# A selective scan fed from GpSimd: one product per unit over both of its pairs, stores of y two units later, one tile of sums for the whole program

## The chip, the cores and the metric

The program runs on one core of one Trainium2 chip. The metric is the device time of one execution in microseconds. The kernel before takes 13546.32 us (median of 3 runs, 13542.6 to 13555.92). A profiled execution of the same kernel took 13547.65 us, of which 13545.9 us lie between its first and its last instruction (the span).

A core has five instruction streams that run side by side and meet only at semaphores: PE (TensorE, matrix products), DVE (VectorE), ACT (ScalarE), POOL (GpSimd) and SP (SyncE, which here issues every DMA). Each stream works in order: an instruction that waits holds up all that stand behind it on its engine.

## The reference: what is computed

The input x is 16 images of 256 channels by 32 x 32 places. Layer 0 adds a transformer block (group norm, layer norms, attention of 4 heads, a GELU layer). Layer 1 adds a Mamba block with a gate. What this change touches is the scan in layer 1:

```python
def step(h, inp):
    d_t, B_t, C_t, u_t = inp
    dA = jnp.exp(d_t[..., None] * A)
    h = dA * h + (d_t * u_t)[..., None] * B_t[:, None, :]
    y = jnp.einsum('bdn,bn->bd', h, C_t)
    return (h, y)
```

It runs over 1024 places for 512 inner channels with 64 states each, for every image: `h` has 512 x 64 values, and at each place it is multiplied by a decay, gets the product (d_t u_t) B_t added, and is summed against C_t over the 64 states to give y.

## The kernel before, in words

**Units.** The scan of one image is cut into 256 units (line 38): two blocks of 512 places (t), four blocks of 128 channels (k), four groups in each (q), eight units in a group (i). A unit has two pairs, e = 0 and 1; the 128 partitions of a pair hold 64 states of 2 channels, and its 512 columns are the places. There are 16 x 256 = 4096 units. I call the group of eight units (b, t, k, q) a group.

For a unit n five things happen:

- `load(n)` (line 838, the DMA at line 859): SP issues one DMA of 512 KB that brings d_t u_t of the unit's channels from DRAM to the tile `dub`, 128 x 2 x 512, each row spread over 64 partitions. `dub` has 7 buffers (`dutp`).
- `inputs(n)` (line 865): GpSimd multiplies each half `dub[:, e, :]` by `bt` (B of the block t, 128 x 512) in place, in two instructions of 128 x 512 (line 869).
- `decay(n)` (line 871): PE forms the exponents in PSUM (line 878), ACT takes the exponential (line 881) into the tiles `a`, of which there are four, that is two units' worth.
- `scan(n, e)` (line 883): VectorE runs the recurrence as one `tensor_tensor_scan` per pair (line 891), from `a` in PSUM and the half of `dub`, into `h`.
- `outputs` (line 915), once per group: PE multiplies `h` by C (`cd`) into the left half of the PSUM tile `yb` (line 928), ACT copies it to `y2` (936), PE turns it into the right half of `yb` (940), ACT copies that to `yo` (948), SP stores it to DRAM in four DMAs of 16 KB (954). It is a generator: it is advanced by one `yield` per unit, so that its parts are spread over the units of the next group. The first part runs at the unit with i = 0, the stores at that with i = 6.

**The loop** over units (from line 974) writes the instructions of one unit after the other: `load(n + 6)`, `inputs(n + 4)`, the two scans of n, `decay(n + 2)`, a share of the side work, then one step of `outputs`. Each compute engine is held to this order (the loop at line 1059 ties every instruction to the one before it on its engine); SP's order follows it closely.

**Side work.** While image b is scanned, the next image is prepared a step at a time: `first_norm`, `attention_layer` and `scan_inputs` of b + 1, and `gate_and_store` of b - 1. The steps are spread evenly over the 256 units. Some of their VectorE instructions read two operands from SBUF: lines 330 (add the position), 515 and 539 (attention), 584, 642 and 682 (the convolution and its gate), 787 and 791 (the gate on y). Others have one operand in PSUM.

**The turn from one image to the next.** At the unit with (k, q, i) = (0, 0, 6) `spread_c` lays out C: GpSimd clears the tile `cd` (128 x 4096, line 903, at t = 0 only), and ACT then writes 8 strided pieces into it (line 907). In GpSimd's order the clearing stands behind the products up to unit 10 of the new image. In ACT's order the exponential for the first group norm of the following image (line 261) stands behind the pieces of `cd`, and VectorE's line 264 needs that exponential.

**Sums.** `yb` (128 x 512 in PSUM, one buffer) is allocated anew for each (b, t), 32 times, and its right half is cleared by VectorE each time (line 918), since PE writes only 16 of every 32 rows of it.

The last image has no following image to prepare: beside its scan only `gate_and_store` of image 14 runs.

Of the kernel before, what the change touches and what calls it, by code (L numbers as in the profile page):

```python
# [11 lines left out]
F32 = mybir.dt.float32  # L12
BF16 = mybir.dt.bfloat16
AF = mybir.ActivationFunctionType
ALU = mybir.AluOpType
# [4 lines left out]
P = 128  # L20
# [3 lines left out]
HL = 512  # L24
# [9 lines left out]
TB = 512  # L34
# [18 lines left out]
def attention_then_scan_kernel(  # L53
# [18 lines left out]
    nc = tc.nc  # L72
    B = x.shape[0]

    def pool(name, bufs, **kw):
        return ctx.enter_context(tc.tile_pool(name=name, bufs=bufs, **kw))
# [13 lines left out]
    yps = pool("yps", 1, space=PSUM)  # L90
# [11 lines left out]
    def work(name, n=L):  # L102
        return wide.tile([P, L + 2 + CONV], F32, name=name, tag="wide")[:, :n]
# [12 lines left out]
    def col(name, i=0, n=1):  # L116
        o, w = _COLS[name]
        assert i + n <= w
        return vec[:, o + i : o + i + n]
# [59 lines left out]
    t = work("ones_s")[:1]  # L179
# [3 lines left out]
    for k in range(KC):  # L183
        t = work("rel_s").rearrange("p (i j) -> p i j", j=32)
        rh = col("rel_h", 32 * k, 32).unsqueeze(1).to_broadcast([P, 32, 32])
        rw = col("rel_w", 32 * k, 32).unsqueeze(2).to_broadcast([P, 32, 32])
        nc.vector.tensor_copy(t, rh)
        nc.vector.tensor_tensor(t, t, rw, ALU.add)
        nc.sync.dma_start(rel[ts(k, P), :], t)


    def weights(*specs):
# [643 lines left out]
    blocks, loaded, decays = {}, {}, {}  # L836
    now = {}
# [26 lines left out]

    def inputs(n):
        b, t = units[n][:2]
        for e in range(2):
            v = loaded[n][:, e, :]
            nc.gpsimd.tensor_tensor(v, v, blocks[b, t]["bt"], ALU.mult)  # L869

    def decay(n):
        b, t, k, q, i = units[n]
# [40 lines left out]


    def outputs(b, t, k, q):
        if (k, q) == (0, 0):
            now["yb"] = yps.tile([P, HL], F32, name="yb", tag="yb")
            nc.vector.memset(now["yb"][:, 256:], 0.0)  # L918
        cd, yb, hbuf = now["cd"], now["yb"], now["h", q % 2]
        out4 = yb[:, 256:].rearrange("p (j a m e) -> p a e j m", a=2, j=2, e=4)  # L920
        if t == 0:
            nc.scalar.copy(now["last"][:, ds(64 * k + 16 * q, 16)], hbuf[:, :, TB - 1])
        for half in range(2):
            for s in range(4):
                for c in range(4):
                    for g in range(4):
                        at = 128 * s + 64 * half + 16 * g + 4 * c
                        nc.tensor.matmul(  # L928
                            yb[ts(g, 32), ts(s, 64)],
                            cd[:, at // 16, ts(c, 32)], hbuf[:, :, at : at + 4],  # L930
                            start=(c == 0), stop=(c == 3),
                        )
                if s == 1:
                    yield
            y2 = blk.tile([P, 256], F32, name="y2", tag="y2")
            nc.scalar.copy(y2, yb[:, :256])  # L936
            yield
            for e in range(4):
                for s in range(4):
                    nc.tensor.matmul(  # L940
                        out4[32 * s : 32 * s + 16, half, e],
                        y2[:, 64 * s + e : 64 * s + 64 : 4], turn[:, e],
                        start=True, stop=True,
                    )
            if half == 0:
                yield
        yo = blk.tile([P, 256], F32, name="yo", tag="yo")
        nc.scalar.copy(yo, yb[:, 256:])
        yield
        to = state[b]["ys"][ds(k * P + 32 * q, 32), ts(t, TB)].rearrange(  # L950
            "(j i) (s c) -> s i j c", j=2, s=4
        )
        for s in range(4):
            nc.sync.dma_start(  # L954
                to[s], yo[32 * s : 32 * s + 16].rearrange("p (j c) -> p j c", j=2)
            )
# [10 lines left out]
    for n in range(LEAD):  # L967
        inputs(n)
# [4 lines left out]
    for n, (b, t, k, q, i) in enumerate(units):  # L973
# [19 lines left out]
        if n + LEAD < len(units):  # L993
            inputs(n + LEAD)
# [11 lines left out]
        if i == 0 and n > 0:  # L1006
            g = outputs(*units[n - 1][:4])
            next(g)
            running.append(g)
# [5 lines left out]
    for _ in outputs(*units[-1][:4]):  # L1015
        pass
# [71 lines left out]
```

## Time and profile before

| | |
|---|---|
| median of 3 runs | 13546.32 us |
| profiled execution | 13547.65 us |
| its span | 13545.9 us |
| VectorE busy | 12092.7 us, 89% |
| PE busy | 10672.8 us, 79% |
| GpSimd busy | 10483.0 us, 77% |
| ScalarE busy | 7925.4 us, 59% |
| mean granted TensorE clock | 0.766 |
| GpSimd products, line 869 | 8192 of 1.307 us |
| scans, line 891 | 8192 of 1.202 or 1.261 us |

How to read it. The first scan starts 388 us into the span: before that the first image is prepared with nothing beside it. From there 15 images take 801 to 836 us each, 3.2 us a unit, and the last image 676 us; 46 us follow the last scan. The busy share of an engine counts instructions from start to end; instructions that follow each other directly on VectorE and GpSimd overlap in the record, so that two scans, of 1.2 us each, are written down as 2.3 to 2.46 us for both. A product that waits for its port is written down as a longer product.

### The profile page before, as it was taken

What the parts mean: (1) busy time and instruction counts of PE and PEld (TensorE: products, weight loads), DVE (VectorE), ACT (ScalarE), POOL (GpSimd) and SP (SyncE); (2) the same over time, 40 slices, a digit from 0 to 9 for tenths busy, and PEclk for the clock granted to TensorE, in tenths of its full rate; (3) what the DMA queues carried; (4) which work ended last, traced back from release to release, by engine and by line L of the source; (5) the groups of instructions that cost most, each with busy time, mean ns of one, the idle gap of its engine ahead of it and who ended that gap; (6) DMA issues with size and microseconds to landing.
All of it is one profiled execution on the core that took longest, in us unless ns stands there. A gap on an engine that the chain in (4) does not pass through costs nothing. (4 is left out here: it accounts for less than half of the span.)

```text
span 13545.9 us, 437083 instructions
## 1 busy us (share of the span) xinstructions
PE 10672.8 (79%) x186800; PEld 5381.9 (40%) x186800; DVE 12092.7 (89%) x11683; ACT 7925.4 (59%) x13941; POOL 10483.0 (77%) x8214
## 2 busy tenths in 40 slices
PE   7787878878787787877878778787887878878757
PEld 3344344433444334443344434434343343433434
DVE  3899999899998989989898998999988999899898
ACT  3666665656656566655656646566565665656644
POOL 0687878878787787877878778787887877878788
PEclk8786877868688686876868778687786877868767
DMA  1566566665666656656666666656666566665666
GB/s 60 198 208 235 196 215 217 205 229 200 208 217 202 228 200 219 210 202 222 207 230 197 204 219 210 232 195 207 220 204 229 197 215 214 201 231 202 203 218 225
DMA packets 1001958, 2821.36 MB, mean 208 GB/s; under 512 B 175810, under 2 KB 319427, under 8 KB 1000004
## 3 DMA queue, kind: packets, MB, share of 16 engines
q1 hardware_dynamic: 1000004, 2793.39, 61.1%
q8 instruction: 1460, 23.92, 0.7%
q14 instruction: 494, 4.05, 0.1%
HBM read 2514.18 MB, written 261.62 MB: 205 GB/s over the span
## 5 line engine op out<-in xcount | busy, mean ns | idle before, releaser
L869 POOL TENSOR_TENSOR dub<-dub,bt 128x512 f32<-128x512 f32 x8192 | 10428.0, 1307 | 3013.2 <-DMA dub<-dus 2609.3
L881 ACT ACTIVATE a<-a,acol 128x512 f32<-128x512 f32 x8192 | 5070.3, 660 | 3815.8 <-PE a L878 3783.7
L891 DVE TENSOR_TENSOR_SCAN h<-a,last,dub 128x512 f32<-128x512 f32 x4096 | 4928.7, 1261 | 136.2 <-POOL dub L869 76.9
L891 DVE TENSOR_TENSOR_SCAN h<-a,dub 128x512 f32<-128x512 f32 x4096 | 4695.9, 1202 | 287.8 <-POOL dub L869 209.5
L878 PE MATMUL a<-pieces,pick 48*128 48x512 bf16 x8192 | 2967.8, 466 | 2345.9 <-DVE h L891 2265.8
L928 PEld LDWEIGHTS yb<-h,cd 128*32 128x32 f32 x131072 | 2563.5, 135 | 2036.9 <-issue 1671.6
L928 PE MATMUL yb<-h,cd 128*32 128x64 f32 x131072 | 2963.2, 258 | 148.9 <-DVE yb L918 108.3
L878 PEld LDWEIGHTS <-pick 48*128 48x128 bf16 x8192 | 520.9, 96 | 2514.6 <-issue 2312.0
L403 PE MATMUL s_ps<-k,q 32*64 32x512 f32 x4096 | 889.3, 717 | 59.1 <-DVE mx L384 57.9
L940 PEld LDWEIGHTS yb<-turn,y 128*16 128x16 f32 x32768 | 408.8, 119 | 1010.9 <-ACT y L936 473.1
L936 ACT COPY y<-yb 128x256 f32<-128x256 f32 x1024 | 383.7, 375 | 728.9 <-PE yb L928 722.9
L384 DVE TENSOR_REDUCE mx<-s_ps 128x1 f32<-128x512 f32 x1024 | 646.1, 675 | 23.6 <-PE s_ps L403 21.5
L940 PE MATMUL yb<-turn,y 128*16 128x32 f32 x32768 | 538.9, 212 | 107.0 <-ACT y L936 97.2
L471 PE MATMUL st_ps<-sp 33*128 33x512 f32 x2048 | 601.1, 632 | 16.7 <-ACT pt L479 15.0
L459 PE MATMUL av<-pt,vv 128*64 128x512 f32 x2048 | 582.7, 648 | 5.6 <-ACT sums L448 3.3
L479 ACT ACTIVATE pt<-st_ps 128x512 f32<-128x512 f32 x1024 | 557.4, 605 | 48.7 <-PE st_ps L471 47.1
L657 PE MATMUL g_ps<-w,xp 128*128 128x256 f32 x1536 | 447.4, 446 | 0.0
L403 PEld LDWEIGHTS s_ps<-k,q 32*64 32x64 f32 x4096 | 207.0, 148 | 580.3 <-DVE mx L384 541.5
L657 PEld LDWEIGHTS g_ps<-w,xp 128*128 128x128 f32 x1536 | 388.9, 328 | 98.6 <-issue 75.0
L816 PE MATMUL m_ps<-w,xs 128*128 128x256 f32 x1024 | 310.5, 452 | 12.0 <-DVE xs L791 12.0
L642 DVE SCALAR_TENSOR_TENSOR u<-up,cwh,u 128x1024 f32<-128x1024 f32 x192 | 285.0, 1485 | 31.8 <-ACT u L634 31.5
L816 PEld LDWEIGHTS m_ps<-w,xs 128*128 128x128 f32 x1024 | 258.8, 328 | 89.8 <-issue 61.4
(135 smaller groups left out, 7122.9 us busy)
## 6 DMA issues: line engine op xcount, KB each, us to landing
dub<-dus SPq DMA_DIRECT2D x4096, 512.0 KB
dps<-pc SPq DMA_DIRECT2D x384, 128.0 KB
pieces<-dps SPq DMA_DIRECT2D x1024, 48.0 KB
xs<-in_x_dram SPq DMA_DIRECT2D x64, 512.0 KB
xs<-kept SPq DMA_DIRECT2D x64, 512.0 KB
zs<-z SPq DMA_DIRECT2D x64, 512.0 KB
ud<-u SPq DMA_DIRECT2D x64, 512.0 KB
dus<-du SPq DMA_DIRECT2D x64, 512.0 KB
```

The costliest lines, as they stand in the source:

```text
L384: nc.vector.tensor_reduce(mx[:, g, c, hf : hf + 1], s, AX.X, ALU.max)
L403: nc.tensor.matmul(waiting[g][0][ts(e, 64)], q4[r, ts(c, 64)], k4[r, hs(hf)], start=True, stop=True,)
L459: nc.tensor.matmul(av[ts(e, 2 * DH)], vv[j // (NJ // 2)][:, j % (NJ // 2), 2 * pair + e, :], pts[e], start=(j == 0), stop=(j == NJ - 1),)
L471: nc.tensor.matmul(s, ka[r, ts(j, P)], qa[r, hs(hf)], start=True, stop=True)
L657: nc.tensor.matmul(ps[:, ts(q, C)], xp[k][:, ds(first + t, P, 4)], wg_s[:, k, t, :], start=(i == 0), stop=False,)
L816: nc.tensor.matmul(ps[:, ts(q, C)], us[d][:, ds(first, P, 4)], wo_s[:, d, :], start=(d == 0), stop=(d == ND - 1),)
L869: nc.gpsimd.tensor_tensor(v, v, blocks[b, t]["bt"], ALU.mult)
L878: nc.tensor.matmul(a, w, pieces[r], start=True, stop=True)
L881: nc.scalar.activation(a, a, AF.Exp, scale=acol[:, at : at + 1])
L891: nc.vector.tensor_tensor_scan(now["h", q % 2][:, 2 * i + e, :], decays[n][e], loaded[n][:, e, :], first, ALU.mult, ALU.add,)
L928: nc.tensor.matmul(yb[ts(g, 32), ts(s, 64)], cd[:, at // 16, ts(c, 32)], hbuf[:, :, at : at + 4], start=(c == 0), stop=(c == 3),)
L940: nc.tensor.matmul(out4[32 * s : 32 * s + 16, half, e], y2[:, 64 * s + e : 64 * s + 64 : 4], turn[:, e], start=True, stop=True,)
```

## The change

Three edits. `inputs` issues one product of 128 x 1024 for the unit, with `bt` read twice through a broadcast, where it issued two of 128 x 512. The stores of y come two units later (with i = 0 of the group after, ahead of the next `outputs`). `yb` is allocated and cleared once, ahead of everything, in place of 32 times.

```diff
+    yb = yps.tile([P, HL], F32, name="yb", tag="yb")
+    nc.vector.memset(yb, 0.0)
...
     def inputs(n):
         b, t = units[n][:2]
-        for e in range(2):
-            v = loaded[n][:, e, :]
-            nc.gpsimd.tensor_tensor(v, v, blocks[b, t]["bt"], ALU.mult)
+        v, bt = loaded[n], blocks[b, t]["bt"]
+        nc.gpsimd.tensor_tensor(v, v, bt.unsqueeze(1).to_broadcast([P, 2, TB]), ALU.mult)
...
     def outputs(b, t, k, q):
-        if (k, q) == (0, 0):
-            now["yb"] = yps.tile([P, HL], F32, name="yb", tag="yb")
-            nc.vector.memset(now["yb"][:, 256:], 0.0)
-        cd, yb, hbuf = now["cd"], now["yb"], now["h", q % 2]
+        cd, hbuf = now["cd"], now["h", q % 2]
...
         yo = blk.tile([P, 256], F32, name="yo", tag="yo")
         nc.scalar.copy(yo, yb[:, 256:])
-        yield
+        for _ in range(3):
+            yield
         to = state[b]["ys"][ds(k * P + 32 * q, 32), ts(t, TB)].rearrange(
```

## The prediction

> **What bounds the kernel now.** I read the busy times first, then the costliest groups of VectorE and GpSimd, and then, since shares are averages, the order of time at places where one of them idles.
>
> ```profile
> PE 10672.8 (79%) x186800; PEld 5381.9 (40%) x186800; DVE 12092.7 (89%) x11683; ACT 7925.4 (59%) x13941; POOL 10483.0 (77%) x8214
> ...
> L869 POOL TENSOR_TENSOR dub<-dub,bt 128x512 f32<-128x512 f32 x8192 | 10428.0, 1307 | 3013.2 <-DMA dub<-dus 2609.3
> L891 DVE TENSOR_TENSOR_SCAN h<-a,last,dub 128x512 f32<-128x512 f32 x4096 | 4928.7, 1261 | 136.2 <-POOL dub L869 76.9
> L642 DVE SCALAR_TENSOR_TENSOR u<-up,cwh,u 128x1024 f32<-128x1024 f32 x192 | 285.0, 1485 | 31.8 <-ACT u L634 31.5
> ```
>
> VectorE is the bound: of 3.2 us a unit the two scans take 2.3 to 2.46, side work most of the rest. GpSimd has idle time and spends it waiting for loads. By the starts and ends in the trace the product of a unit is complete 12.5 us (median, first 15 images) before its scan starts. So the waits that the list puts down to GpSimd (286.3 us, VectorE's line 891 on line 869) mostly belong to others, and a faster product is worth nothing in the middle of an image. Two places are different.
>
> The first is the turn between images, here to image 5, from the order of time on GpSimd, ACT and VectorE:
>
> ```profile
> 4490.32 44.23 POOL L869 TENSOR_TENSOR dub<-dub,bt 128x512 f32<-128x512 f32 x36 [5.85 <-DMA dub<-dus]
> 4534.47 3.53 POOL L903 MEMSET cd<- 128x4096 f32 x1
> ...
> 4538.03 2.45 ACT L907 ACTIVATE cd<-ct,par 128x128 f32<-128x128 f32 x8 [3.08 <-POOL cd L903]
> ...
> 4544.65 1.22 DVE L264 TENSOR_TENSOR gn<-gn,gn_v_ps 128x1024 f32<-128x1024 f32 x1 [6.03 <-ACT gn_v_ps L261]
> ```
>
> Columns are start, length, instruction, and in brackets the idle time before. GpSimd runs 36 products (18 units) without a pause, clears `cd`, ACT stood 3.08 us for that, and VectorE 6.03 us for ACT. Here GpSimd's pace ends last.
>
> The second is VectorE's instructions with two SBUF operands:
>
> ```profile
> L642 DVE SCALAR_TENSOR_TENSOR u<-up,cwh,u x192: 1250/1274/2374, 282.5 to 12642.2; 128x1024 f32<-128x1024 f32 x192
> ...
> L787 DVE SCALAR_TENSOR_TENSOR xs<-xs,vec x64: 1253/1588/16045, 1245.4 to 13522.4; 128x1024 f32<-128x1024 f32 x64
> ```
>
> ```profile
> 5967.20 1.26 POOL L869 TENSOR_TENSOR dub<-dub,bt 128x512 f32<-128x512 f32 x1
> 5967.49 2.06 DVE L642 SCALAR_TENSOR_TENSOR u<-up,cwh,u 128x1024 f32<-128x1024 f32 x1
> 5968.43 2.26 POOL L869 TENSOR_TENSOR dub<-dub,bt 128x512 f32<-128x512 f32 x1
> ```
>
> The same instruction takes 1.25 us alone (minimum) and up to 2.37 (maximum). In the example it starts 0.97 us before the first product of a unit ends, and ends 1.09 us after that; the second product, begun 0.03 us before the first ends, stretches to 2.26 us. The two engines exclude each other, one instruction at a time, and VectorE gets in **between the two products of a unit**. Line 787's 16 us are another case: four times in the last image it stood behind 12 products in a row, with GpSimd never idle.
>
> ```profile
> 12911.84 15.74 DVE L787 SCALAR_TENSOR_TENSOR xs<-xs,vec 128x1024 f32<-128x1024 f32 x1
> ...
> 12908.12 18.38 POOL L869 TENSOR_TENSOR dub<-dub,bt 128x512 f32<-128x512 f32 x15
> ```
>
> What this exclusion costs now: counts times (mean less minimum) over lines 642, 682, 787, 791, 584, 330, 539 and 515 come to 200 us. Of that four waits of line 787 are 58, and 142 us are ordinary, over 508 instructions, 0.28 us each.
>
> **The change part by part.** The sum is made against the profiled execution, 13547.65 us, 1.3 above the median.
>
> *Length of the merged product.* No row shows 128 x 1024 on GpSimd. Products in a row start 1.226 us apart (44.23 us for 36). Merging saves the fixed part of one instruction. Its shortest instruction, a clearing of one column, takes 0.099 us; its 128-column select takes 0.295, which also holds work on columns. So a merged product takes 2.35 us against 2.45, with ends of 2.16 and 2.45 (nothing saved). I take 2.35: the one-column row is nearest to a pure fixed part. The Trainium skill (GPSIMD Engine Reference, Elementwise) gives 4497 ns for a two-input add of 2048 columns; with the row's 1.27 us for 512 columns an estimate from that page is 2.30 us apart, and the next term would be -41 in place of -27.
>
> *Turns between images.* 18 units times 0.099 us is 1.8 us off the run of products, the clearing comes earlier by that, and with it ACT and VectorE's line 264, or in the last image the scan of its unit 9. ACT waited 62.5 us for the clearing in 15 turns, 4.2 on average, so 1.8 fits in. 15 x 1.8 = **-27 us**; ends 0 and -62. The first scan of a unit now waits for both halves; at the turns the second half ends at worst 0.6 us after the scan's start, and by then the run is 0.7 us ahead, so this costs nothing (at most 15 x 0.6 = 9).
>
> *Exclusion.* An instruction of VectorE that arrives in the first product of a unit gets in after it today; merged, it waits for what was the second as well. By starts and ends in the trace, images 0 to 14 have 472 such instructions: 63 arrive with no product running, 252 in the second product of a unit, 157 in the first. Only the 157 change. All of them with 1.12 us more (the second product less the fixed part) would be 176 us. But 79 of them arrive in the last 0.2 us of the first product: there a run of two products began when the previous such instruction let go, and two scans (2.46) took about as long as the run (2.45). After the merge such a run is one whole product, 2.35 us, and ends before the scans do, so these arrive free. The other 78 pay 1.1 us: **+85 us**, all on the path, as VectorE is the bound. Ends 0 (arrivals all fall in step with the products' ends) and +176. I take the middle value, since it is counted from this trace. The Trainium skill (SBUF, "two separate sides") says the same and speaks against the change: the port pair is an exclusive lock for the whole instruction, the loser fully blocks. By that rule alone, with arrivals at random, the mean wait would go with the product's length, 0.28 to 0.52 us, or +122 us.
>
> *The four long waits.* Between them VectorE's unit takes 2.23 us and GpSimd's 2.45, so GpSimd falls behind and has six units of landed loads to run through. Falling behind by 0.12 instead of 0.22 us a unit, over the some 22 units before each, leaves it one unit less to run, about 2.4 us, and 0.1 for each of the others: 4 x 3 = **-12 us**; ends 0 and -54.
>
> *The tile of sums.* 32 clearings of 0.272 us go, one of 128 x 512 comes (0.485, the row of line 429), in VectorE's order: **-8 us**; ends 0 and -9. PE's 108.3 us of waiting for it (14 times) goes too, but no scan waits for PE there.
>
> *The stores of y.* SP waits 557.6 us for line 948 at the stores; two units later that wait is gone, and loads behind it are issued up to 3 us sooner. The product's lead of 12.5 us hides that today: 0. At the turn the four stores (1.7 us of SP) now stand ahead of the load that starts the run of 36, but SP idles there from 2803.5 to 2807.2 us in the turn to image 3, waiting for line 748. If that cover were gone: 15 x 1.7 = +26. `yo` has two buffers, so its next copy waits for nothing new.
>
> The sum is -27 + 85 - 12 - 8 + 0 = +38 us: 13547.65 + 38, about **13585 us**, 0.29% over the median.
>
> **The rivals.**
> 1. *Exclusion costs nothing more* (faster). VectorE's arrivals settle just after the products' ends, as the medians close to the minimum (1274 against 1250 for line 642) suggest. Against it: means of 1485 and 1497 show that a quarter to a half of them don't. Then -47: 13501 us, and down to 13423 with the other terms at their ends. It decides when the added wait is under about 20 us.
> 2. *VectorE loses the port for a further product.* An arrival within the last 0.1 us of a product already loses to the next one today (the maxima of 2.37 us); a loss would then cost 2.35 us. If half of some 170 arrivals near an end lose, 85 x 2.35 = 200 in place of 85: about 13700 us. Against it: GpSimd mostly has no next load landed (1593 waits for loads).
> 3. *Nothing measurable*: the terms cancel, the exclusion costing 20 to 70 us: 13520 to 13573.
> 4. *The product gets no shorter, or longer*: the -27 and -12 go, 13625 us; at 3.2 us a product or more GpSimd would bound everything.
>
> **How the numbers follow.** A measurement of this kernel can tell about 0.2% (27 us) from no change. I give the forecast with its neighbours above 13573 a chance of 0.40, rival 1 0.27, rival 2 0.12, rival 3 0.18, rival 4 0.03. So faster 0.27, same 0.18, slower 0.55. The range reaches from below rival 1 (its likely part, 13480) to rival 2 (13700); below it and above it I leave about 0.1 each. The forecast's own range, with the exclusion between 60 and 120 us, is 13560 to 13620.
>
> **What would show each step.** In the profile after: 4096 products of about 2.4 us (their mean, with waits, near 2.5); the idle time before line 264 on ACT down from 96.2 us by some 25; the minima of lines 642, 682, 787, 791 unchanged, their means up by 0.15 to 0.3 us and line 642's maximum near 3.5; line 787's longest near 13 us; line 918 once; SP's wait on line 948 near zero. I am wrong if those means don't rise, if the merged product is under 2.23 us (then GpSimd keeps pace in the last image and the four long waits go), or if VectorE's idle time before scans grows.

## The result, and the profile after

The changed kernel takes 13529.56 us (median of 12 runs, 13499.69 to 13552.05) beside 13544.95 for the kernel before in the same session: ratio 0.9988, 95% interval 0.998 to 0.9997. It is about 15 us faster, where 39 us slower was forecast; the range held it, the likeliest case did not. Its profiled execution took 13520.45 us (span 13518.5), 27.2 less than that of before.

In the changed file the quoted side lines stand three lower (642 is 645, 787 is 790, 264 is 267, 515 is 518); the product is line 871, the scan 893, the load 862.

From the page of the kernel after, the busy times and three of the costliest groups:

```profile
PE 10686.8 (79%) x186800; PEld 5389.6 (40%) x186800; DVE 12165.9 (90%) x11652; ACT 7916.0 (59%) x13941; POOL 9761.5 (72%) x4118
...
L871 POOL TENSOR_TENSOR dub<-dub,bt 128x1024 f32<-128x1024 f32 x4096 | 9706.4, 2386 | 3702.5 <-DMA dub<-dus 3218.5
...
L645 DVE SCALAR_TENSOR_TENSOR u<-up,cwh,u 128x1024 f32<-128x1024 f32 x192 | 341.0, 1776 | 32.8 <-ACT u L637 32.5
```

GpSimd does the same work in 722 us less. VectorE is busier, 12165.9 against 12092.7 us: line 645 alone has 56 us more (341.0 against 285.0).

Two-operand lines of VectorE, shortest, median and longest in ns:

```profile
L645 DVE SCALAR_TENSOR_TENSOR u<-up,cwh,u x192: 1250/1522/3484, 271.7 to 12644.1; 128x1024 f32<-128x1024 f32 x192
```

```profile
L790 DVE SCALAR_TENSOR_TENSOR xs<-xs,vec x64: 1250/1768/11680, 1233.4 to 13495.4; 128x1024 f32<-128x1024 f32 x64
```

The minima stand, the medians and the maximum of line 645 rose (1274 to 1522, 2374 to 3484): a merged product is waited for whole. Line 790's longest fell from 16.0 to 11.7 us.

The turn to image 5, from the order of time on GpSimd:

```profile
4488.78 41.62 POOL L871 TENSOR_TENSOR dub<-dub,bt 128x1024 f32<-128x1024 f32 x18 [6.51 <-DMA dub<-dus]
```

18 units take 41.62 us, 2.312 each, where they took 44.23.

VectorE's list of waits (us in total, times, longest), first of the kernel before, then of the kernel after:

```profile
DVE gn L264 <- ACT gn_v_ps L261: 96.2, 16, 7.9
...
DVE ao L515 <- DMA sums<-den: 56.4, 15, 5.5
```

```profile
DVE gn L267 <- ACT gn_v_ps L264: 61.8, 16, 5.3
...
DVE ao L518 <- DMA sums<-den: 11.2, 10, 5.6
```

The first pair is the turn between images, 34 us less. The second pair is in none of the prediction's steps: `ao`, the attention's output divided by its softmax sums, waits 45 us less for these sums to arrive. That is more than the whole difference between the two kernels.

By stages (times between the first scans of the images): before the first scan -10.8 us, images 0 to 14 +11.9, the last image -29.0, after it +0.6. The start-up of the kernels below, in which next to nothing of it is changed, stands -2 to +16 us to that of before from trace to trace; what the -10.8 comes from no run here shows.

What happened around `ao` is read from SP's queue in image 5, where the sums of the softmax are put through DRAM: `den` is written, `few` read, inverted by VectorE, `den` written again, and read into `sums`. First before, then after (start, length, DMAs that SP issues):

```profile
5763.28 0.55 SPq L496 DMA_DIRECT2D few<-den  x1
5764.68 1.71 SPq L954 DMA_DIRECT2D ys<-yo  x4
5766.43 0.52 SPq L859 DMA_DIRECT2D dub<-dus  x1
5768.19 0.34 SPq L505 DMA_DIRECT2D den<-few  x1
5770.47 2.87 SPq L859 DMA_DIRECT2D dub<-dus  x2
5773.43 1.93 SPq L508 DMA_DIRECT2D sums<-den  x4
```

```profile
5759.35 0.55 SPq L499 DMA_DIRECT2D few<-den  x1
5761.10 0.52 SPq L862 DMA_DIRECT2D dub<-dus  x1
5761.71 0.55 SPq L954 DMA_DIRECT2D ys<-yo  x1
5764.35 0.34 SPq L508 DMA_DIRECT2D den<-few  x1
5764.74 0.89 SPq L954 DMA_DIRECT2D ys<-yo  x2
5766.66 0.52 SPq L862 DMA_DIRECT2D dub<-dus  x1
5767.27 1.93 SPq L511 DMA_DIRECT2D sums<-den  x4
```

Before, two loads of `dub` stand between `den` and `sums`; after, one load and two stores. A load waits for a scan to free its buffer, so each costs SP about a unit: `sums` is issued 5.24 us after `den` before (5768.19 to 5773.43), 2.92 us after. VectorE meanwhile, of before:

```profile
5767.81 0.35 DVE L503 RECIPROCAL few<-few 128x32 f32<-128x32 f32 x1 [2.81 <-DMA few<-den]
...
5780.72 0.75 DVE L515 TENSOR_TENSOR ao<-ao,sums 128x512 f32<-128x512 f32 x1 [3.00 <-DMA sums<-den]
```

and of after:

```profile
5763.97 0.35 DVE L506 RECIPROCAL few<-few 128x32 f32<-128x32 f32 x1 [2.93 <-DMA few<-den]
...
5774.48 0.75 DVE L518 TENSOR_TENSOR ao<-ao,sums 128x512 f32<-128x512 f32 x1 [0.84 <-DMA sums<-den]
```

Eight scans lie between the two instructions in both kernels. Before, they do not cover the way of the sums (3.00 us idle); after, they nearly do (0.84). Of the other 14 such places, 13 have the same two orders of SP.

### The profile page after: what moved, and what is told of

The parts are those of the page before. It is cut to its first block, busy times and chain, and to the rows that moved or that the text cites. A ratio compares the mean times of both kernels' runs of the same rounds, so it can differ in the third digit from the quotient of the medians.

```text
span 13518.5 us, 429250 instructions
## 1 busy us (share of the span) xinstructions
PE 10686.8 (79%) x186800; PEld 5389.6 (40%) x186800; DVE 12165.9 (90%) x11652; ACT 7916.0 (59%) x13941; POOL 9761.5 (72%) x4118
## 5 line engine op out<-in xcount | busy, mean ns | idle before, releaser
L871 POOL TENSOR_TENSOR dub<-dub,bt 128x1024 f32<-128x1024 f32 x4096 | 9706.4, 2386 | 3702.5 <-DMA dub<-dus 3218.5
L939 PE MATMUL yb<-turn,y 128*16 128x32 f32 x32768 | 538.2, 212 | 103.2 <-ACT y L935 99.4
L645 DVE SCALAR_TENSOR_TENSOR u<-up,cwh,u 128x1024 f32<-128x1024 f32 x192 | 341.0, 1776 | 32.8 <-ACT u L637 32.5
```

The source lines that it names most:

```text
L871: nc.gpsimd.tensor_tensor(v, v, bt.unsqueeze(1).to_broadcast([P, 2, TB]), ALU.mult)
L939: nc.tensor.matmul(out4[32 * s : 32 * s + 16, half, e], y2[:, 64 * s + e : 64 * s + 64 : 4], turn[:, e], start=True, stop=True,)
```

## The experiments

"Ordinary exclusion" below is, as in the prediction, the duration over the minimum, summed over the eight two-operand lines, without waits over 2.5 us ("long waits"), which are counted apart. Before: 142.5 us ordinary, 57.8 in 4 long waits. After: 257.9 and 27.3 in 3.

**One edit alone, and the three with one undone.** e1: only the stores late.

```diff
         nc.scalar.copy(yo, yb[:, 256:])
-        yield
+        for _ in range(3):
+            yield
```

> The kernel before with the stores of y two units later and nothing else. Theory A: this edit moves SP's order in the attention's softmax sums, so that one load fewer stands between the store of the reciprocals and the four loads of the sums; VectorE's wait at line 515 falls from 56.4 us to about 12, and the time by 38 to 45 us, to some 13505 (ratio 0.997). Theory B, that of the prediction: SP's time is hidden, and the time stays (ratio 1.000).

Measured: ratio 0.9973 (0.9963 to 0.9983). VectorE's wait for the sums, in place of the 56.4 us of before:

```profile
DVE ao L515 <- DMA sums<-den: 10.2, 9, 5.5
```

By its trace `ao`'s idle time in images 0 to 14 went from 50.8 to 4.7 us, and these images together are 41.4 us shorter than before (the last image is 20.6 longer, on which more at e4). The stores alone give the gain, and more than the whole change.

e2: only the product merged.

```diff
-        for e in range(2):
-            v = loaded[n][:, e, :]
-            nc.gpsimd.tensor_tensor(v, v, blocks[b, t]["bt"], ALU.mult)
+        v, bt = loaded[n], blocks[b, t]["bt"]
+        nc.gpsimd.tensor_tensor(v, v, bt.unsqueeze(1).to_broadcast([P, 2, TB]), ALU.mult)
```

> The kernel before with the merged product and nothing else. Theory A: +97 us of exclusion in images 0 to 14, -34 us at the turns, -29 us in the last image: +34 us, 13579 (ratio 1.0025), and the wait at line 515 stays at 56 us. Theory B: the longer VectorE instructions cost nothing, because what follows them would have waited anyway, and the freed GpSimd gives the whole gain: -15 to -60 us (ratio 0.996 to 0.999), with line 515's wait down to 11 us as in the changed kernel.

Measured: 1.0047 (1.0032 to 1.0061). Its profiled execution is the slowest of its six, 26 us over their median; in it images 0 to 14 are 103.2 us longer than before, the last image 29.3 shorter. Three lines of its trace, the line of the convolution and two waits:

```profile
L642 DVE SCALAR_TENSOR_TENSOR u<-up,cwh,u x192: 1249/1554/3386, 298.3 to 12761.8; 128x1024 f32<-128x1024 f32 x192
```

```profile
DVE gn L264 <- ACT gn_v_ps L261: 57.9, 16, 5.3
...
DVE ao L515 <- DMA sums<-den: 55.4, 15, 5.6
```

Both halves of the reasoning on the product are in it: line 642 longer (+63 us with its idle time), the turn shorter (96.2 to 57.9), and `ao` as it was. The merged product by itself makes the kernel slower, as forecast.

e3: only one tile of sums (the first and third hunk of the change).

> The kernel before with one tile of sums for the whole program and nothing else. Both theories: -8 to -10 us (ratio 0.9993), no VectorE wait changed. If it is more, PE's 108 us of waiting for the clearing were on the path.

Measured: 1.0003 (0.9991 to 1.0014). In its trace the clearings (10.4 us with their idle time) are gone; in the time that isn't resolved.

e4: the whole change with the product in two again.

```diff
-        v, bt = loaded[n], blocks[b, t]["bt"]
-        nc.gpsimd.tensor_tensor(v, v, bt.unsqueeze(1).to_broadcast([P, 2, TB]), ALU.mult)
+        for e in range(2):
+            v = loaded[n][:, e, :]
+            nc.gpsimd.tensor_tensor(v, v, blocks[b, t]["bt"], ALU.mult)
```

> The changed kernel with the two products of 128x512 put back. Theory A: only the stores and the tile of sums are left, -38 to -45 and -10: 13490 to 13500 us (ratio 0.9963), faster than the changed kernel by some 35 us; the means of the two-operand VectorE lines back at 1.48 to 1.50 us. Theory B: slower than the changed kernel, 13535 to 13545 us.

Measured: 0.9974 (0.9964 to 0.9983); ordinary exclusion 141.9 us. So within the change the merge costs about 0.0014 of the time (0.9988 against 0.9974; by the two intervals between about 0 and 0.0027), some 19 us, where e2 shows 0.0047, 64 us. Put otherwise, the three edits alone add up to 1.0023, and together they measure 0.9988: 0.0035 apart, where the four intervals, taken together by their squares, allow 0.0023. The terms of the traces go the same way (ordinary exclusion +146 us in e2, +116 in after against e4; the turns -38 and -32; line 787 with its idle time -31 and -33), but the two whole traces do not help: that of after is 15 us shorter than that of e4, whose profiled execution is 19 us over the median of its runs.

A part of the difference shows in the last image. With two products per unit it takes 685.7 to 696.4 us in the traces with late stores (e1, e4, e10), with 6 or 7 long waits of 69 to 79 us together, and 675.7 to 679.8 us in those without (before, e3, and e9 below, which has them in one group), with 4 or 5 long waits of 58 to 62 us. With the merged product it takes 646.4 and 646.7 us (e2, after). So late stores cost some 10 to 20 us there, which the merge takes away again. Why the merge is dearer alone by the rest of the 45 us stays open: exclusion is 30 us higher there, and why that is no run shows.

**The stores: one place, or SP everywhere?** e1 leaves a second reading: late stores free SP from 557.6 us of waiting for ACT's `yo`, so that loads might come earlier everywhere. Of the 32 groups of an image, only one, (t, k, q) = (0, 3, 3), has its stores beside the softmax's sums. e9 moves the stores of this group alone, e10 those of all others.

```diff
         nc.scalar.copy(yo, yb[:, 256:])
-        yield
+        for _ in range(3 if (t, k, q) == (0, 3, 3) else 1):
+            yield
```

> The kernel before, with the stores of y of one group of an image alone, that of (t, k, q) = (0, 3, 3), issued two units later; the other 31 groups store as before. That group's stores are the ones whose turn comes while the sums of the attention go through DRAM. Theory that the gain of the stores is SP's order at that one place: the whole gain is here. SP's order becomes few, load, store, den, two stores, load, four sums; VectorE's idle time before line 515's ao on the DMA of sums falls from about 50 us to about 5 in images 0 to 14, ratio 0.997 (about -40 us). Rival, that later stores free SP everywhere and loads come earlier all through an image: 1/32 of the gain, ratio 1.000 within 0.001.

e10 has `1 if (t, k, q) == (0, 3, 3) else 3`.

> The kernel before, with the stores of y issued two units later in all groups of an image but that of (t, k, q) = (0, 3, 3). Theory that the gain is SP's order at that one place: none here, ratio 1.000 within 0.001, VectorE's idle time before line 515's ao stays at about 50 us, although SP's waits for line 948 go nearly as far down as with all stores late. Rival, that later stores free SP everywhere: nearly the whole gain, ratio 0.997.

Measured: e9 0.9961 (0.9948 to 0.9975), e10 0.9998 (0.9989 to 1.0006). SP's wait for `yo` before:

```profile
SPq L954 <- ACT yo L948: 557.6, 282, 12.0
```

VectorE's wait for the sums and SP's for `yo`, of e9:

```profile
DVE ao L515 <- DMA sums<-den: 8.9, 7, 5.8
```

```profile
SPq L955 <- ACT yo L948: 546.3, 265, 12.0
```

and of e10:

```profile
DVE ao L515 <- DMA sums<-den: 58.4, 15, 5.7
```

```profile
SPq L955 <- ACT yo L948: 78.1, 57, 12.5
```

This tells the two readings apart. e9 keeps nearly all of SP's waiting and has the whole gain; e10 takes most of SP's waiting away and gains nothing. SP's 557.6 us hid behind the product's lead, as forecast, save for the one place where something other than a load stood behind it.

**The merged product where GpSimd's pace ends last, two products elsewhere.** e5: stores late, one tile of sums, and

```diff
+        at = n % UNITS
+        if b + 1 == B or at <= 10 or at >= UNITS - 7:
+            v = loaded[n]
+            nc.gpsimd.tensor_tensor(v, v, bt.unsqueeze(1).to_broadcast([P, 2, TB]), ALU.mult)
+        else:
             for e in range(2):
...
```

> Stores late, one tile of sums, and the merged product only where GpSimd's pace ends last: units 249 to 10 around each turn and the whole last image; two products of 128x512 everywhere else. If the merged product's gain lies at the turns and in the last image and its cost in the middle of the images (exclusion): -34 us at the turns and -30 to -39 us in the last image against the version with two products throughout (0.9974), so a ratio of about 0.992 to the kernel before, with the two-operand VectorE lines at their means of before. If the gain does not depend on the place, it comes out between that version and the changed kernel, 0.997 to 0.999.

Measured: 13441.74 us (4 runs), 0.9908 (0.9894 to 0.9921): faster than both kernels. The convolution's line, and the wait at the turn:

```profile
L645 DVE SCALAR_TENSOR_TENSOR u<-up,cwh,u x192: 1250/1276/2378, 280.2 to 12561.5; 128x1024 f32<-128x1024 f32 x192
```

```profile
DVE gn L267 <- ACT gn_v_ps L264: 58.8, 16, 4.9
```

Line 645 is back at its median of before, ordinary exclusion is 136.6 us, and the turn has the merged product's gain. Against the trace of e4 it is 93 us shorter: the turns 35, the last image 34 (28 of it line 790 with its long waits), the start-up 3, and several small pieces in images 0 to 14.

**Smaller products.** If a wait lasts for one product, products half as long as before should halve it. e6: after with four products of 128 x 256 for a unit.

```diff
+        for e in range(2):
+            for f in range(2):
+                v = loaded[n][:, e, ts(f, TB // 2)]
+                nc.gpsimd.tensor_tensor(v, v, blocks[b, t]["bt"][:, ts(f, TB // 2)], ALU.mult)
```

> The changed kernel with four products of 128x256 per unit. If VectorE gets in at the end of each product, its two-operand lines come down: line 642's mean from 1485 ns (two products) and 1776 (one) to about 1370 and its maximum to about 1.9 us. With a fixed part of 0.1 us each, a unit takes GpSimd some 2.65 us, so the run of 18 units at the turn is 3.6 us longer (+54 us over 15 turns) and the last image, bound by GpSimd, 50 to 60 us longer: ratio about 1.000 to 1.003. If the exclusion is by the run of products and not by the instruction, the means stay at 1485 or rise.

Measured: 1.0234 (1.0218 to 1.025), a miss. Its profiled execution took 22039.1 us, with PE busy for 20623.0 us, where the other three took 13867.86 to 13893.18; so only its times are used here. e7 has the four products only where e5 has two.

> As the version with the merged product at the turns and in the last image, but with four products of 128x256 in the middle of the images in place of two. If the wait is what is left of the running product: half of the some 145 us of ordinary exclusion goes, -60 to -75 us, ratio about 0.987 to 0.988. If it is by the run of products: no faster than with two, 0.992.

Measured: 1.0057 (1.0044 to 1.0071), a miss again, by 1.9% of the time. Its groups of GpSimd's products, and the line that took most of the time:

```profile
L879 POOL TENSOR_TENSOR dub<-dub,bt 128x256 f32<-128x256 f32 x14280 | 10241.6, 776 | 1582.8 <-DMA dub<-dus 1391.0
...
L518 DVE TENSOR_TENSOR ao<-ao,sums 128x512 f32<-128x512 f32 x32 | 236.2, 7384 | 12.6 <-DMA sums<-den 12.6
```

Line 518 needs 33.6 us for its 32 instructions in e5 (1052 ns each), here 236.2. One of them, beside GpSimd, in order of time:

```profile
5702.34 148.20 POOL L879 TENSOR_TENSOR dub<-dub,bt 128x256 f32<-128x256 f32 x216 [0.18 <-DMA dub<-dus]
```

```profile
5834.19 16.90 DVE L518 TENSOR_TENSOR ao<-ao,sums 128x512 f32<-128x512 f32 x1 [0.76 <-DMA sums<-den]
```

A product of 128 x 256 starts 0.684 us after the last, four take 2.74 us, and in that stretch a unit of VectorE is two scans, 2.35 to 2.46 us. GpSimd falls behind, never pauses for 148 us, and VectorE is kept out for 16 us, over some 23 products, as line 787 was in the last image of before. The ordinary waits gain little: 126.3 us against 136.6, not half. They do get shorter, but there are more of them: in images 0 to 14, 359 instructions of the eight lines lose over 0.1 us, 0.33 us each on average, where in e5 225 lose 0.56 us each. GpSimd's products fill 86% of these images, against 79% in e5. And of the 139 that start in the last 0.2 us of a product, 87 lose over 0.5 us, that is the next product as well (14 of 198 in e5). Here the fixed part of the smaller products also makes GpSimd's pace the bound in the stretches that consist of scans alone.

**What exclusion costs in all.** e8 leaves the product with B out altogether (the scan then adds d_t u_t, not d_t u_t B_t), otherwise it is after.

> The changed kernel without GpSimd's product with B (this part of the computation is left out; all else stays). Prices the exclusion by itself: with no products, all eight two-operand VectorE lines should stand at their minima (line 642 at 1.25 us), -285 us against the changed kernel, and ACT's and VectorE's wait for the clearing at the turns (61.8 us) go in part: 13180 to 13220 on the scale of 13530, ratio about 0.975 to the kernel before. If waits elsewhere take the place of the exclusion, the means fall but the ratio stays above 0.99.

Measured: 0.9818 (0.9804 to 0.9831), less than expected. Its two lines:

```profile
L645 DVE SCALAR_TENSOR_TENSOR u<-up,cwh,u 128x1024 f32<-128x1024 f32 x192 | 242.2, 1262 | 32.6 <-ACT u L637 32.4
L790 DVE SCALAR_TENSOR_TENSOR xs<-xs,vec 128x1024 f32<-128x1024 f32 x64 | 81.7, 1277 | 83.8 <-DMA xs<-ud 83.4
```

and the second of them in after:

```profile
L790 DVE SCALAR_TENSOR_TENSOR xs<-xs,vec 128x1024 f32<-128x1024 f32 x64 | 138.6, 2166 | 40.0 <-DMA xs<-ud 40.0
```

Every wait is gone (6.6 us left of 285.2), so these stretched instructions are GpSimd's doing and nothing else's. The time falls by 204 us against the trace of after, although the start-up is 12 us longer; 19 us of the fall are the turns' (the wait of line 267 goes from 61.8 to 43.0). So some 197 us are left for the 279 us of waits: about 0.7 of exclusion's price is on the path. The rest comes back as idle time: line 790 now stands 44 us longer for its load (83.8 us against 40.0), and the scans' idle time is 23 us longer, nearly all of it now for ACT.

## Why the prediction was wrong

**The failed step: "The product's lead of 12.5 us hides that today: 0"**, said of the stores of y. It measured -45 us in the trace (`ao`, 56.4 to 11.3), and 0.9973 and 0.9961 in e1 and e9. The cover was named for one customer of SP only, the loads of `dub`, and for these it was true (e10). But moving four DMAs in SP's queue against the loads also moves everything else there, and the sums of the softmax stand there with a consumer on VectorE, the bound. The row was to be seen: `ao`'s wait of 56.4 us for `sums<-den` is in the list of waits of before, with a DMA as its releaser, and the one load fewer before `sums` is in the new program's order. Put in place of the 0, the sum is 38 - 45 = -7 us: the sign of the result, though not for certain its size, since the merge, forecast at 85 - 27 - 12 = +46 us, costs 64 us alone and some 19 beside the other edits (e4). The prediction did ask what the four stores do to the load at the turn, and bounded that with +26; nothing of that kind shows (the turn is shorter by what the product gives).

The other steps, each against its own term:

- *Length of the merged product*: 2.31 us, taken as 2.35. The fixed part is 0.140 us, not 0.099: three sizes start 0.684, 1.226 and 2.311 us apart, which is 0.140 us + 2.12 ns a column. The Trainium skill's 4497 ns at 2048 columns (GPSIMD Engine Reference, Elementwise) lies on this line (4.48), and its 2.30 us was the better estimate.
- *Turns*: -27 taken, -34 measured. 15 x 18 x 0.140 is 38. Right, a little small.
- *Exclusion*: +85 taken, +115 measured (142.5 to 257.9), inside its ends. "These arrive free" is what was too favourable: in images 0 to 14, of the 472 instructions those that start in the last 0.2 us of a running product fell from 192 to 76, those that lose over 0.1 us rose from 224 to 271, and their mean loss from 0.61 to 0.92 us. What VectorE had fallen in step with was not kept.
- *The four long waits*: -12 taken, -30 measured (57.8 to 27.3; three remain, the longest instruction 11.7 us where 13 was said). In the traces with two products throughout they come 4 to 7 times, 58 to 79 us in all, and with merged products in the last image 3 times, 25 to 32 us.
- *The tile of sums*: -8 taken, -10 in the trace, in the time nothing that could be resolved (e3).

With the five measured terms the sum is -34 + 115 - 30 - 10 - 45 = -4 against -27 in the two profiled executions. VectorE does its work in one order, so the traces can be added up without overlap, each instruction counted from the end of the one before it. In images 0 to 14 the eight two-operand lines are 110 us longer; `ao`'s wait is 45 shorter, the turns 34, the scans' idle time 12, the clearings 10; small pieces make +3, together the +11.9. The last image is 29.0 us shorter, all of it at line 787. What the five terms lack is thus the start-up's -10.8 and the scans' idle time, which the prediction had no term for.

Of the rivals, 1 (exclusion costs nothing more) named the right side for a reason that is false: e2 has +146 us of it, and is slower. Rival 2 (a further product lost) is out: of the instructions that start in the last 0.2 us of a product, 16 lost over 0.5 us before and none after. Rival 4 is out by the merged product's 2.31 us. Rival 3's 13520 to 13573 has the measured time in it, and the terms do cancel, but not as it put it: exclusion costs 115, not 20 to 70, and what cancels it is above all the term that was set to 0. Of the named signs, the rise of line 642's mean (1485 to 1776), its maximum near 3.5 (3.48) and 34 us off line 264's wait came as said; SP's wait for line 948 went to 56.9, not to zero. The means of lines 682 and 791 rose by 0.38 and 0.16 us; that of line 787 fell (2551 to 2166 ns), as its long waits did. The signs of being wrong all watched the product and the idle time before the scans; none watched the term of the stores, and so none could show the step that failed.

## What to carry to other kernels

When a step is moved past others in an in-order DMA queue, list each thing that stands behind it there, and for each who waits for it on the bounding engine; cover that holds for the main stream of loads says nothing of the rare round trip beside it (here 14 places, some 3 us each, together more than the whole change gained). The length of an instruction on an engine that excludes another is a choice per stretch, not per program: long where its pace ends last, short where the other engine must get in (e5, 0.9908), and not so short that its fixed part lets it fall behind (e7, 1.0057).

## What was unexpected of the hardware

VectorE can be kept out by GpSimd for much longer than the instruction that is running. The Trainium skill (SBUF, "two separate sides") has the port pair as a lock for a whole instruction; most ordinary waits fit that, one running product and then VectorE's turn (those that lose the next product too, 16 before and 87 in e7, do not). But waits of 13 to 15 us occur over 11 or 12 further products of 128 x 512 (before, line 787), 7 to 10 us over 2 to 4 of 128 x 1024 (after), 11 to 17 us over 16 to 25 of 128 x 256 (e7, line 518). In all traces here they come only when GpSimd has run for 13 us or more, with 12 products or more done, without a pause, and such a run does not always bring one (before has 58 instructions of these lines that start 15 us or more into a run and wait for less than 2.5 us). What then decides between a wait of one product and a long one no run here shows; the end of such a wait was not explained either.
